# A^T and score rows by block transposes and GpSimd-issued DMAs, and the softmax tied to a later sum, in a two-layer graph kernel

## The chip, the cores and the metric

The kernel runs on one core of a Trainium2 chip. The metric is the time of one execution in device microseconds (us). Three runs of the kernel before gave 2418.76, 2420.62 and 2421.0; the median is 2420.62.

## What is computed

There are 128 graphs of 128 nodes with 512 features. Layer 0 is attention with three powers of a transition matrix; layer 1 weighs each node by a softmax over the nodes. Cut to what matters (`aw[:d]` and `aw[d:]` are the two halves of `aw`):

```python
h = relu(layernorm(x))                                   # layer 0
Xw = h @ Wv + bv
sj, si = Xw @ aw[:d], Xw @ aw[d:]
e = leaky_relu(sj[:, None, :] + si[:, :, None] + ab, 0.2)
alpha = A * exp(e)
T = alpha / (sum(alpha, -1) + 1e-12)
H, Xk = 0, h
for k in range(3):
    H = H + Xk @ Wk[k] + bk[k]
    Xk = T @ Xk
x = x + relu(H)
h = relu(layernorm(x))                                   # layer 1
q, k = split(h @ Wqk); v = h @ Wv1
w = (q * (A @ (k * mask))).sum(-1) * mask / sqrt(512)
x = x + softmax(w, over nodes)[:, :, None] * v
```

## The kernel before, in words

The graphs are worked two at a time (G = 2): 64 pairs, nodes on the 128 partitions. Both layers' large products are Strassen products of seven parts, where the two graphs of a pair are the two row halves. In layer 0 (`strassen0`, L356) a part is six matmuls of 256 columns; in layer 1 (`strassen1`, L387) it is two matmuls of 512 columns. The parts run in the order 1, 6, 7, 5, 2, 3, 4. They are summed in three PSUM banks (a, b and c in the code), and VectorE evicts intermediate sums between the parts (L366 to L381, and L398 to L408), each of which has to be read before a later part writes on into its bank. All matmuls of the two run from the helper at L346.

One turn of the loop (L476) holds layer 0 of pair p and layer 1 of pair p-1. In the middle of layer 0, `steps[0]` (called behind L369) brings in pair p+1: the feature transposes (`begin`, L271), `attention` (L274), and `finish` of layer 1 (L426) for the pair that ended last; `steps[1]` (called behind L374) brings `t_transposed` (L304). After layer 0 come `propagate` (L317, matmuls L325), the norm of layer 1's input, layer 1's product, `aggregate` (L411, matmul L417, sum L420), the left-hand sums (`left_sums`, L329), and at the end of the turn the norm and the score sums (L255) of pair p+2.

Three small jobs in that turn go through TensorE's transpose:

- `attention` needs the score of the neighbours as a row on every partition. `spread` (L97) transposes a column that is broadcast over 128 columns; there is one for each graph, into PSUM, from where VectorE reads it at L282.
- `attention` transposes A (L298); ScalarE scales the result by the mask at L302 on its way out of PSUM.
- `finish` spreads the column w of layer 1 in the same way (L97) and takes the maximum (L431) and two exponentials (L434) from it.

An operation goes to the engine that the code names; a scheduler decides the order on each engine when the program is built, by the order of the code and by when it takes operands to be ready. On the chip, each engine works down its own list. All loads and stores inside the loop are issued by SP, among them the pair's features written to DRAM and read back in blocks (hd, hv, L258 to L266), so that VectorE's 32x32 block transposes (L271) complete a transpose. GpSimd issues no DMA.

Buffers: four PSUM banks for the products and four for the rest, three sets of loaded inputs, two of most tiles in front, one of the tiles in `late`.

Of the kernel before, what the change touches and what calls it, by code (L numbers as in the profile page):

```python
# [8 lines left out]
FP = mybir.dt.float32  # L9
# [6 lines left out]
def kernel(  # L16
# [20 lines left out]
    nc = tc.nc  # L37
# [25 lines left out]

        return bass.AP(tensor=ap.tensor, offset=ap.offset + offset, ap=[[0, P], [1, n]])

    xg, ag = {}, {}

    def load(p):
        s = slice(p * G, (p + 1) * G)
        xg[p] = loads.tile([P, G, D], FP, name="xg")  # L70
        nc.sync.dma_start(xg[p], x[s].rearrange("b n d -> n b d"))
        ag[p] = loads.tile([P, G, N], FP, name="ag")
        nc.sync.dma_start(ag[p], adj[s].rearrange("b n m -> n b m"))


    nc.scalar.preload_act_table_set("natural_log_exp_and_others")
# [159 lines left out]
                                 bias=rs[:, 1, j:j + 1], scale=rs[:, 0, j:j + 1])  # L236
        return h

    H, HV, S, X, SX, AT, T, TT, X1, H2, X2, SX2 = ({} for _ in range(12))

    def norm0(p):

# [5 lines left out]
    def score_sums(p):  # L248

        h = H[p]  # L250
        s = S[p] = small.tile([P, G, 2], FP, name="s")
        for j in range(G):
            for a in range(2):
                junk = front.tile([P, D], FP, name="junk", bufs=1)
                nc.vector.scalar_tensor_tensor(junk, h[:, j, :], 1.0, u_bc[:, a, :], op0=OP.mult,  # L255
                                               op1=OP.mult, accum_out=s[:, j, a:a + 1])

    def by_blocks(h):  # L258

# [8 lines left out]
    def transposed(hv, dst):  # L268

        for j in range(G):  # L270
            nc.vector.transpose(dst[:, j].rearrange("p f (n b) -> p f n b", n=Q),  # L271
                                hv[:, j].rearrange("p n (f a) -> p f n a", f=Q))

    def attention(p):  # L274

        a, s = ag.pop(p), S.pop(p)
        pz = ps_t.tile([P, DC, P], FP, name="pt")
        for j in range(G):
            spread(pz[:, j, :], s[:, j, 0:1])
        z = front.tile([P, G, N], FP, name="z", bufs=1)  # L280
        for j in range(G):
            nc.vector.tensor_scalar(z[:, j, :], pz[:, j, :], s[:, j, 1:2], cz, op0=OP.add, op1=OP.add)  # L282
        nc.vector.scalar_tensor_tensor(z, z, 0.2, z, op0=OP.mult, op1=OP.max)
        ex = front.tile([P, G, N], FP, name="ex")
        nc.scalar.activation(ex, z, AF.Exp)
        d = small.tile([P, 2, G], FP, name="d")
        for j in range(G):
            nc.vector.scalar_tensor_tensor(ex[:, j, :], ex[:, j, :], 1.0, a[:, j, :], op0=OP.mult,
                                           op1=OP.mult, accum_out=d[:, 0, j:j + 1])
        nc.vector.tensor_scalar(d[:, 0], d[:, 0], 1e-12, None, op0=OP.add)  # L290
        nc.vector.reciprocal(d[:, 1], d[:, 0])
        t = T[p] = front.tile([P, G, N], FP, name="t")
        for j in range(G):
            nc.vector.tensor_scalar(t[:, j, :], ex[:, j, :], d[:, 1, j:j + 1], None, op0=OP.mult)

        pa = ps_t.tile([P, DC, P], FP, name="pt")
        for j in range(G):
            nc.tensor.transpose(pa[:, j, :], a[:, j, :], ident)  # L298
        AT[p] = front.tile([P, G, N], FP, name="aT", bufs=3)
        for j in range(G):  # L300
            b = p * G + j
            nc.scalar.activation(AT[p][:, j, :], pa[:, j, :], AF.Copy, scale=maskT[:, b:b + 1])  # L302

    def t_transposed(p):  # L304

        t, tt = T.pop(p), front.tile([P, G, 2, N], FP, name="tt")
        pt = ps_t.tile([P, DC, P], FP, name="pt")
        for j in range(G):
            nc.tensor.transpose(pt[:, j, :], t[:, j, :], ident)  # L309
        nc.scalar.copy(tt[:, :, 0, :], pt[:, :G, :])  # L310
        pt = ps_t.tile([P, DC, P], FP, name="pt")
        for j in range(G):
            nc.tensor.matmul(pt[:, j, :], t[:, j, :], tt[:, j, 0, :], start=True, stop=True)  # L313
        nc.scalar.copy(tt[:, :, 1, :], pt[:, :G, :])
        TT[p] = tt
# [40 lines left out]
    def strassen0(p, steps):  # L356

        product = products(SX.pop(p), right0)
        X.pop(p)
        lo, hi = bsum[:, :HD], bsum[:, HD:]  # L360
        hb = X1[p] = front.tile([P, G, D], FP, name="x1", bufs=3)
        s = front.tile([P, 4, HD], FP, name="s0", bufs=1)
        ba, bb, bc = (ps_m.tile([P, D], FP, name="pm") for _ in range(3))
        a, b, c = ba[:, :HD], bb[:, :HD], bc[:, :HD]
        product(ba, 1, True)
        nc.vector.tensor_add(s[:, 0], a, hi)  # L366
        nc.vector.tensor_add(s[:, 1], a, lo)
        product(bb, 6, True)
        nc.vector.tensor_add(s[:, 2], b, s[:, 1])  # L369
        steps[0]()  # L370
        product(bc, 7, True)
        product(bb, 5, False)
        nc.vector.tensor_add(s[:, 3], b, s[:, 0])
        nc.vector.tensor_add(hb[:, 1, HD:], c, s[:, 3])  # L374
        steps[1]()
        product(ba, 2, False)
        nc.vector.tensor_add(hb[:, 0, :HD], a, lo)
        product(bb, 3, False)
        nc.vector.tensor_add(hb[:, 0, HD:], b, s[:, 0])
        product(bc, 4, False)  # L380
        nc.vector.tensor_add(hb[:, 1, :HD], c, s[:, 2])  # L381
        xs = xg.pop(p)
        for j in range(G):
            nc.vector.scalar_tensor_tensor(hb[:, j, :], hb[:, j, :], 0.0, xs[:, j, :],
                                           op0=OP.max, op1=OP.add)

    def strassen1(p):  # L387

        product = products(SX2.pop(p), R1)
        X2.pop(p)  # L390
        yv = late["p"].tile([P, G, 2, 2, HD], FP, name="yv")
        o = [[yv[:, j, nh].rearrange("p k d -> p (k d)") for nh in range(2)] for j in range(G)]
        s = late["p"].tile([P, 3, D], FP, name="s1")
        a, b, c = (ps_m.tile([P, D], FP, name="pm") for _ in range(3))
        product(a, 1, True)
        nc.scalar.copy(s[:, 0], a)
        product(b, 6, True)
        nc.vector.tensor_add(s[:, 1], b, s[:, 0])  # L398
        product(c, 7, True)
        product(b, 5, False)  # L400
        nc.vector.tensor_add(s[:, 2], b, s[:, 0])
        nc.vector.tensor_add(o[1][1], c, s[:, 2])
        product(a, 2, False)
        nc.scalar.copy(o[0][0], a)
        product(b, 3, False)
        nc.vector.tensor_add(o[0][1], b, s[:, 0])  # L406
        product(c, 4, False)
        nc.vector.tensor_add(o[1][0], c, s[:, 1])  # L408
        return yv

    def aggregate(p, yv):  # L411

        h2, at = H2.pop(p), AT.pop(p)
        w = small.tile([P, 6, G], FP, name="w")
        for j in range(G):
            pa = ps_t.tile([P, D], FP, name="pt")
            nc.tensor.matmul(pa, at[:, j, :], h2[:, j, :], start=True, stop=True)  # L417
            junk = front.tile([P, D], FP, name="junk", bufs=1)
            b = p * G + j
            nc.vector.scalar_tensor_tensor(  # L420
                junk.rearrange("p (k d) -> p k d", k=2), pa.rearrange("p (k d) -> p k d", k=2),
                wscale[:, b:b + 1], yv[:, j, :, 0, :], op0=OP.mult, op1=OP.mult,
                accum_out=w[:, 0, j:j + 1])
        return w

    def finish(p, yv, w):  # L426

        pw = ps_t.tile([P, DC, P], FP, name="pt")
        for j in range(G):
            spread(pw[:, j, :], w[:, 0, j:j + 1])  # L430
        nc.vector.tensor_reduce(w[:, 1], pw[:, :G, :], AX.X, OP.max, negate=True)  # L431
        for j in range(G):
            ej = front.tile([P, N], FP, name="ej")
            nc.scalar.activation(ej, pw[:, j, :], AF.Exp, bias=w[:, 1, j:j + 1],  # L434
                                 accum_out=w[:, 2, j:j + 1])
        nc.vector.tensor_add(w[:, 3], w[:, 0], w[:, 1])
        nc.scalar.activation(w[:, 4], w[:, 3], AF.Exp)
        nc.vector.reciprocal(w[:, 5], w[:, 2])
        nc.vector.tensor_mul(w[:, 3], w[:, 4], w[:, 5])
# [29 lines left out]
    R1 = None  # L469
    ends = []  # L470

    def end():
        while ends:
            finish(*ends.pop())

    for p in range(NP + 1):  # L476
        if p < NP:
            if p + 1 < NP:
                n = p + 1
                steps = (lambda: (begin(n), attention(n), end()), lambda: t_transposed(n))  # L480
            else:
                steps = (end, lambda: None)
            strassen0(p, steps)
            if p + 1 < NP:
                propagate(p + 1)
# [7 lines left out]
        if p < NP:  # L493
            H2[p] = norm_relu(X1[p], "h2", late["p"])
            hv2 = by_blocks(H2[p])
        if p > 0:
            yv = strassen1(p - 1)
            w = aggregate(p - 1, yv)
        if p + 1 < NP:
            prepare0(p + 1)  # L500
        if p > 0:
            ends.append((p - 1, yv, w))
        if p < NP:
            X2[p] = late["p"].tile([P, G, 2, HC, N], FP, name="x2")
            transposed(hv2, X2[p].rearrange("p j h c n -> p j (h c) n"))
            a = {(j, kh): X2[p][:, j, kh:kh + 1].rearrange("p k c n -> p k (c n)")
                 for j in range(G) for kh in range(2)}
            SX2[p] = left_sums(a, late["p"], "sx2", [1, HD])
        if p + 2 < NP:
            norm0(p + 2)  # L510
            score_sums(p + 2)
    end()


# [23 lines left out]
```

## Time and profile before

| | |
|---|---|
| median of 3 runs | 2420.62 us |
| the profiled execution, its own time | 2420.37 us |
| its span in the profile | 2418.3 us |
| mean granted TensorE clock | 0.998 |
| VectorE (DVE) busy | 1786.8 us, 74% |
| ScalarE (ACT) busy | 650.5 us, 27% |
| GpSimd (POOL) busy | 0.7 us |
| DMA engines, 0 to 20 us, and 20 to 60 us | 0.89 and 0.71 busy |
| mean DMA rate | 91 GB/s |

The span runs from the first to the last instruction in the trace of one execution; the time of that execution is a little longer. PE is TensorE's matmuls and PEld its weight loads, which lie beside them. A line such as "L346 PE MATMUL pm<-t,sx" names the line of the code, the engine, the operation, and the tiles written and read. A row of the chain of waits names what the end of the run hung on at that time.

### The profile page before, as it was taken

How to read it: one execution, taken by the hardware profiler on the slowest of the kernel's cores; microseconds unless marked ns; L12 is line 12 of the kernel's file. 1: busy time of each engine (PE TensorE's matmuls, PEld its weight loads, DVE VectorE, ACT ScalarE, POOL GpSimd, SP SyncE). 2: the span in 40 equal slices, each digit the busy share in tenths (PEclk: the TensorE clock that was granted, in tenths of full speed). 3: DMA queues.
4: the chain of work that ended last, by engine and by line, in shares of the span. 5: the costliest groups of instructions: out<-in, count | busy, mean ns of one | idle time of the engine just before them, and what ended most of it. 6: DMA issues, size and time to landing. Idle time of an engine off the chain costs nothing.

```text
span 2418.3 us, 27245 instructions
## 1 busy us (share of the span) xinstructions
PE 2378.8 (98%) x9289; PEld 1694.5 (70%) x9289; DVE 1786.8 (74%) x4768; ACT 650.5 (27%) x1557; POOL 0.7 (0%) x6
## 2 busy tenths in 40 slices
PE   6999999999999999999999999999999999999997
PEld 4777677677676676776776776776766767767764
DVE  6777777777777777777777777777777777777764
ACT  3222222222222222223222222222222222232221
POOL 0000000000000000000000000000000000000000
PEclk9999999999999999999999999999999999999999
DMA  7233233233133233232332332332332332323311
GB/s 219 82 84 101 81 92 101 66 106 101 64 109 93 71 101 95 77 101 88 85 101 81 92 100 65 108 100 64 108 93 72 101 95 78 100 87 86 97 52 52
DMA packets 236986, 220.48 MB, mean 91 GB/s; under 512 B 14384, under 2 KB 170160, under 8 KB 236848
## 3 DMA queue, kind: packets, MB, share of 16 engines
q1 hardware_dynamic: 232624, 216.65, 30.5%
q10 hardware_dynamic: 4224, 2.10, 0.3%
q8 instruction: 73, 1.20, 0.2%
q14 instruction: 65, 0.53, 0.1%
HBM read 118.03 MB, written 100.66 MB: 90 GB/s over the span
## 4 chain that ended last, share of the span: by engine, by line
PE 96%; DVE 2%; DMA 1%; issue 0%; ACT 0%; SPq 0%; DVEq 0%; ACTq 0%
PE pm L346 79%; PE pt L325 9%; PE pt L417 4%; PE pt L97 1%; PE pt L313 1%; PE pt L298 1%; PE pt L309 1%; DMA bk_bc<-in_L_gnn_bk_dram 0%; DMA hd<-h 0%; DVE st L220 0%; DMA hv<-hd 0%; DMA w<-in_L_gnn_Wqk_dram 0%; DMA xg<-in_x_dram 0%; DVE x L271 0%; PE pm L208 0%
## 5 line engine op out<-in xcount | busy, mean ns | idle before, releaser
L346 PE MATMUL pm<-t,sx 128*128 128x256 f32 x2304 | 518.6, 380 | 1.4 <-DVE sx L333 1.4
L346 PEld LDWEIGHTS pm<-t,sx 128*128 128x128 f32 x2304 | 433.4, 190 | 57.4 <-DVE sx L333 2.0
L346 PE MATMUL pm<-b,x 128*128 128x256 f32 x1536 | 363.0, 380 | 0.0
L346 PE MATMUL pm<-f,sx 128*128 128x512 f32 x768 | 344.8, 598 | 0.3
L346 PEld LDWEIGHTS pm<-b,x 128*128 128x128 f32 x1536 | 282.6, 191 | 59.3 <-issue 29.6
L327 ACT COPY x<-pt 128x512 f32<-128x512 f32 x256 | 148.7, 581 | 500.6 <-PE pt L325 500.6
L346 PEld LDWEIGHTS pm<-f,sx 128*128 128x128 f32 x768 | 141.6, 191 | 193.7 <-issue 154.4
L346 PE MATMUL pm<-e,x 128*128 128x512 f32 x512 | 242.5, 596 | 6.5 <-DVE x L271 6.5
L325 PE MATMUL pt<-tt,h 128*128 128x256 f32 x1024 | 231.5, 379 | 0.0
L325 PEld LDWEIGHTS pt<-tt,h 128*128 128x128 f32 x1024 | 194.9, 190 | 26.2
L255 DVE SCALAR_TENSOR_TENSOR junk<-h,u_bc 128x512 f32<-128x512 f32 x256 | 176.4, 689 | 7.8 <-ACT h L235 0.9
L346 PE MATMUL pm<-b,sx 128*128 128x256 f32 x768 | 176.5, 379 | 0.0
L346 PE MATMUL pm<-t,x 128*128 128x256 f32 x768 | 176.2, 379 | 0.0
L235 ACT ACTIVATE h<-x,rs 128x512 f32<-128x512 f32 x128 | 97.2, 806 | 289.9 <-PE pt L417 277.1
L271 DVE STREAM_TRANSPOSE x<-hv 128x512 f32<-128x512 f32 x256 | 166.4, 688 | 6.6 <-DMA hv<-hd 5.7
L346 PEld LDWEIGHTS pm<-e,x 128*128 128x128 f32 x512 | 97.8, 191 | 102.8 <-issue 92.3
L346 PEld LDWEIGHTS pm<-t,x 128*128 128x128 f32 x768 | 146.2, 190 | 19.6
L346 PEld LDWEIGHTS pm<-b,sx 128*128 128x128 f32 x768 | 146.0, 190 | 19.5
L406 DVE TENSOR_TENSOR yv<-pm,s 128x512 f32<-128x512 f32 x64 | 44.3, 692 | 128.5 <-PE pm L346 128.5
L235 ACT ACTIVATE h<-xg,rs 128x512 f32<-128x512 f32 x128 | 97.2, 806 | 119.8 <-DVE rs L232 119.8
L417 PE MATMUL pt<-h,aT 128*128 128x512 f32 x256 | 120.5, 593 | 0.5 <-ACT h L235 0.5
L346 PE MATMUL pm<-e,sx 128*128 128x512 f32 x256 | 120.3, 592 | 0.0
(101 smaller groups left out, 2511.3 us busy)
## 6 DMA issues: line engine op xcount, KB each, us to landing
hd<-h SPq DMA_DIRECT2D x128, 512.0 KB, 3.1
hv<-hd SPq DMA_DIRECT2D x512, 128.0 KB, 3.3
xg<-in_x_dram SPq DMA_DIRECT2D x64, 512.0 KB, 3.6
out_dram<-x SPq DMA_DIRECT2D x64, 512.0 KB, 3.1
ag<-in_adj_dram SPq DMA_DIRECT2D x64, 128.0 KB, 3.0
w<-in_L_gnn_Wqk_dram ACTq DMA_DIRECT2D x8, 256.0 KB, 5.0
b<-in_L_gnn_Wk_dram SPq DMA_DIRECT2D x8, 256.0 KB, 3.4
wv_sb<-in_L_gnn_Wv_dram SPq DMA_DIRECT2D x4, 256.0 KB, 5.3
```

Source lines behind the costliest of these rows:

```text
L97: nc.tensor.transpose(dst, col.to_broadcast([P, P]), ident)
L235: nc.scalar.activation(h[:, j, :], src[:, j, :], AF.Relu, bias=rs[:, 1, j:j + 1], scale=rs[:, 0, j:j + 1])
L255: nc.vector.scalar_tensor_tensor(junk, h[:, j, :], 1.0, u_bc[:, a, :], op0=OP.mult, op1=OP.mult, accum_out=s[:, j, a:a + 1])
L271: nc.vector.transpose(dst[:, j].rearrange("p f (n b) -> p f n b", n=Q), hv[:, j].rearrange("p n (f a) -> p f n a", f=Q))
L298: nc.tensor.transpose(pa[:, j, :], a[:, j, :], ident)
L309: nc.tensor.transpose(pt[:, j, :], t[:, j, :], ident)
L313: nc.tensor.matmul(pt[:, j, :], t[:, j, :], tt[:, j, 0, :], start=True, stop=True)
L325: nc.tensor.matmul(pt[:, c].rearrange("p k n -> p (k n)"), h[:, j, at:at + P], tt[:, j].rearrange("p k n -> p (k n)"), start=True, stop=True)
L327: nc.scalar.copy(X[p][:, 1:3, j, kh].rearrange("p k c n -> p c k n"), pt)
L346: nc.tensor.matmul(bank[:, :r.shape[-1]], left[i][:, k, c * P:(c + 1) * P], r, start=(first and at == 0), stop=(at == len(chunks) - 1), sk ...
L406: nc.vector.tensor_add(o[0][1], b, s[:, 0])
L417: nc.tensor.matmul(pa, at[:, j, :], h2[:, j, :], start=True, stop=True)
```

## The change

Every load of a pair also reads A a second time, in blocks of 32x32 (`agb`), by four DMAs that GpSimd issues. One block transpose on VectorE turns it into A^T, and ScalarE scales that in place. The score column and layer 1's column w are kept in zeroed tiles of 128x32 (`cols`); a block transpose makes rows of them, two small DMAs put the rows into DRAM, and one DMA broadcasts them back to all partitions, all three issued by GpSimd (`spread_pair`). Pair 0's scores and the last pair's w still go through TensorE. `norm0` of pair p+2 moves ahead of layer 1's product, and its score sums into the middle of it. In layer 0, `attention` is called one part later (behind part 7's matmuls), `t_transposed` one part later (behind L377), and `finish` writes its maximum into the tile of layer 0's last intermediate sum, `s[:, 3]`, so that it comes behind L374, which reads that sum. Some tiles get one buffer instead of two, and the exponential is taken in place.

```diff
+        agb[p] = loads.tile([P, G, Q, S32], FP, name="agb", bufs=2)
+        v = adj[s].rearrange("g (q b) (c i) -> c b (g q) i", b=S32, i=S32)
+        for c in range(Q):
+            nc.gpsimd.dma_start(agb[p][c * S32:(c + 1) * S32].rearrange("p g q i -> p (g q) i"), v[c])
...
+    cols = [const.tile([P, S32], FP, name=f"col{i}") for i in range(6)]
+    for t in cols:
+        nc.gpsimd.memset(t, 0.0)
...
-        s = S[p] = small.tile([P, G, 2], FP, name="s")
+        s = S[p] = cols[p % 3]
...
+        PZ[p] = spread_pair(s, "pz", p > 0)
...
+    def spread_pair(col, name, by_dma):
+        if by_dma:
+            t = small.tile([P, S32], FP, name=f"{name}t", bufs=1)
+            nc.vector.transpose(t, col)
+            d = dram.tile([G, Q, S32], FP, name=f"{name}d")
+            for j in range(G):
+                nc.gpsimd.dma_start(d[j], t[j::S32])
+            dst = front.tile([P, G, N], FP, name=name, bufs=1)
+            nc.gpsimd.dma_start(dst.rearrange("p g n -> p (g n)"), bcast(d, 0, G * N))
+            return dst
+        pz = ps_t.tile([P, DC, P], FP, name="pt")
+        for j in range(G):
+            spread(pz[:, j, :], col[:, j:j + 1])
+        return pz[:, :G]
...
-        ex = front.tile([P, G, N], FP, name="ex")
+        ex = z
...
-        t = T[p] = front.tile([P, G, N], FP, name="t")
+        t = T[p] = front.tile([P, G, N], FP, name="t", bufs=1)
...
-        pa = ps_t.tile([P, DC, P], FP, name="pt")
-        for j in range(G):
-            nc.tensor.transpose(pa[:, j, :], a[:, j, :], ident)
         AT[p] = front.tile([P, G, N], FP, name="aT", bufs=3)
+        nc.vector.transpose(AT[p].rearrange("p g n -> p (g n)"),
+                            agb.pop(p).rearrange("p g q i -> p (g q i)"))
...
-            nc.scalar.activation(AT[p][:, j, :], pa[:, j, :], AF.Copy, scale=maskT[:, b:b + 1])
+            nc.scalar.activation(AT[p][:, j, :], AT[p][:, j, :], AF.Copy, scale=maskT[:, b:b + 1])
...
-        t, tt = T.pop(p), front.tile([P, G, 2, N], FP, name="tt")
+        t, tt = T.pop(p), front.tile([P, G, 2, N], FP, name="tt", bufs=1)
...
         product(bc, 7, True)
+        steps[1]()
         product(bb, 5, False)
         nc.vector.tensor_add(s[:, 3], b, s[:, 0])
         nc.vector.tensor_add(hb[:, 1, HD:], c, s[:, 3])
-        steps[1]()
+        end(s[:, 3, :G])
         product(ba, 2, False)
         nc.vector.tensor_add(hb[:, 0, :HD], a, lo)
+        steps[2]()
         product(bb, 3, False)
...
         nc.vector.tensor_add(o[1][1], c, s[:, 2])
+        if ahead < NP:
+            score_sums(ahead)
         product(a, 2, False)
...
-        nc.vector.tensor_reduce(w[:, 1], pw[:, :G, :], AX.X, OP.max, negate=True)
+        nc.vector.tensor_reduce(peak, pw, AX.X, OP.max, negate=True)
...
-                steps = (lambda: (begin(n), attention(n), end()), lambda: t_transposed(n))
+                steps = (lambda: begin(n), lambda: attention(n), lambda: t_transposed(n))
...
+        if p + 2 < NP:
+            norm0(p + 2)
         if p > 0:
-            yv = strassen1(p - 1)
+            yv = strassen1(p - 1, p + 2)
+        elif p + 2 < NP:
+            score_sums(p + 2)
+        if p > 0:
             w = aggregate(p - 1, yv)
...
-            ends.append((p - 1, yv, w))
+            ends.append((p - 1, yv, w, spread_pair(w, "pw", p < NP)))
...
-        if p + 2 < NP:
-            norm0(p + 2)
-            score_sums(p + 2)
```

More of the change, by code (lines that the diff above doesn't have):

```diff
@@ L64, in bcast @@
         return bass.AP(tensor=ap.tensor, offset=ap.offset + offset, ap=[[0, P], [1, n]])
-    xg, ag = {}, {}
+    xg, ag, agb = {}, {}, {}
     def load(p):
@@ L237, in norm_relu @@
         return h
-    H, HV, S, X, SX, AT, T, TT, X1, H2, X2, SX2 = ({} for _ in range(12))
+    cols = [const.tile([P, S32], FP, name=f"col{i}") for i in range(6)]
+    for t in cols:
+        nc.gpsimd.memset(t, 0.0)
+    H, HV, S, PZ, X, SX, AT, T, TT, X1, H2, X2, SX2 = ({} for _ in range(13))
     def norm0(p):
@@ L255, in score_sums @@
                 nc.vector.scalar_tensor_tensor(junk, h[:, j, :], 1.0, u_bc[:, a, :], op0=OP.mult,
-                                               op1=OP.mult, accum_out=s[:, j, a:a + 1])
+                                               op1=OP.mult, accum_out=s[:, a * G + j:a * G + j + 1])
+        PZ[p] = spread_pair(s, "pz", p > 0)
     def by_blocks(h):
@@ L272, in transposed, with attention @@
                                 hv[:, j].rearrange("p n (f a) -> p f n a", f=Q))
-    def attention(p):
-        a, s = ag.pop(p), S.pop(p)
+    def spread_pair(col, name, by_dma):
[8 more added lines that the diff above has]
+            return dst
         pz = ps_t.tile([P, DC, P], FP, name="pt")
         for j in range(G):
-            spread(pz[:, j, :], s[:, j, 0:1])
+            spread(pz[:, j, :], col[:, j:j + 1])
+        return pz[:, :G]
+    def attention(p):
+        a, s, pz = ag.pop(p), S.pop(p), PZ.pop(p)
         z = front.tile([P, G, N], FP, name="z", bufs=1)
         for j in range(G):
-            nc.vector.tensor_scalar(z[:, j, :], pz[:, j, :], s[:, j, 1:2], cz, op0=OP.add, op1=OP.add)
+            nc.vector.tensor_scalar(z[:, j, :], pz[:, j, :], s[:, G + j:G + j + 1], cz, op0=OP.add, op1=OP.add)
         nc.vector.scalar_tensor_tensor(z, z, 0.2, z, op0=OP.mult, op1=OP.max)
-        ex = front.tile([P, G, N], FP, name="ex")
+        ex = z
         nc.scalar.activation(ex, z, AF.Exp)
@@ L385, in strassen0, with strassen1 @@
                                            op0=OP.max, op1=OP.add)
-    def strassen1(p):
+    def strassen1(p, ahead):
         product = products(SX2.pop(p), R1)
@@ L413, in aggregate @@
         h2, at = H2.pop(p), AT.pop(p)
-        w = small.tile([P, 6, G], FP, name="w")
+        w = cols[3 + p % 3]
         for j in range(G):
@@ L422, in aggregate, with finish @@
                 wscale[:, b:b + 1], yv[:, j, :, 0, :], op0=OP.mult, op1=OP.mult,
-                accum_out=w[:, 0, j:j + 1])
+                accum_out=w[:, j:j + 1])
         return w
[L426 to L430, printed above, removed]
-        nc.vector.tensor_reduce(w[:, 1], pw[:, :G, :], AX.X, OP.max, negate=True)
+    def finish(peak, p, yv, ws, pw):
+        w = ws[:, :6 * G].rearrange("p (k g) -> p k g", g=G)
+        nc.vector.tensor_reduce(peak, pw, AX.X, OP.max, negate=True)
         for j in range(G):
             ej = front.tile([P, N], FP, name="ej")
-            nc.scalar.activation(ej, pw[:, j, :], AF.Exp, bias=w[:, 1, j:j + 1],
+            nc.scalar.activation(ej, pw[:, j, :], AF.Exp, bias=peak[:, j:j + 1],
                                  accum_out=w[:, 2, j:j + 1])
-        nc.vector.tensor_add(w[:, 3], w[:, 0], w[:, 1])
+        nc.vector.tensor_add(w[:, 3], w[:, 0], peak)
         nc.scalar.activation(w[:, 4], w[:, 3], AF.Exp)
@@ L470, with end @@
     ends = []
-    def end():
+    def end(peak=None):
         while ends:
-            finish(*ends.pop())
+            finish(small.tile([P, G], FP, name="peak") if peak is None else peak, *ends.pop())
     for p in range(NP + 1):
@@ L479 @@
                 n = p + 1
-                steps = (lambda: (begin(n), attention(n), end()), lambda: t_transposed(n))
+                steps = (lambda: begin(n), lambda: attention(n), lambda: t_transposed(n))
             else:
-                steps = (end, lambda: None)
+                steps = (lambda: None,) * 3
             strassen0(p, steps)
```

## The prediction

> **What bounds the kernel now.** I read the busy shares first, then the chain of waits over the whole span and over one pair, then VectorE's timeline of that pair, then the waits.
>
> ```profile
> PE 2378.8 (98%) x9289; PEld 1694.5 (70%) x9289; DVE 1786.8 (74%) x4768; ACT 650.5 (27%) x1557; POOL 0.7 (0%) x6
> ```
> ```profile
> PE 96%; DVE 2%; DMA 1%; issue 0%; ACT 0%; SPq 0%; DVEq 0%; ACTq 0%
> ```
>
> TensorE is busy all the time and is 96% of the chain that ends last. The chain over one pair:
>
> ```profile
> 1031.23 5.18 PE pm L346 x24
> 1036.41 0.22 PE pt L97 x2
> 1036.62 0.22 PE pt L298 x2
> 1036.84 0.22 PE pt L97 x2
> 1037.06 5.18 PE pm L346 x24
> 1042.24 0.22 PE pt L309 x2
> ...
> 1050.68 3.45 PE pt L325 x16
> 1054.13 12.07 PE pm L346 x28
> 1066.21 1.72 PE pt L417 x4
> ```
>
> Columns are start, length and what ran. There is no gap, so a pair costs what TensorE is given: from 1036.41 to 1073.11, where the next pair has the same L97 row, 36.70 us. The three 0.22 us rows are what the change removes.
>
> The other engine that matters is VectorE. In its timeline (start, mean length, operation, idle time before) I look at the first evictions of layer 1:
>
> ```profile
> 1042.28 0.42 DVE L373 TENSOR_TENSOR s<-pm,s 128x256 f32<-128x256 f32 x1 [0.91 <-PE pm L346]
> 1042.74 0.42 DVE L374 TENSOR_TENSOR x<-pm,s 128x256 f32<-128x256 f32 x1
> ...
> 1048.59 0.69 DVE L384 SCALAR_TENSOR_TENSOR x<-x,xg 128x512 f32<-128x512 f32 x1
> ...
> 1058.34 0.68 DVE L398 TENSOR_TENSOR s<-pm,s 128x512 f32<-128x512 f32 x1
> ```
>
> L398's input is ready when layer 1's second product ends, 1054.13 + 2 x 1.72 = 1057.57, but VectorE comes to it at 1058.34, with no idle time named before it. The waits say the same:
>
> ```profile
> PEld pm L346 <- DVE s L398: 38.8, 63, 1.0
> ```
>
> So TensorE's weight load already waits 0.6 us a pair there, and the matmul stream just escapes. VectorE is 74% busy on average, but late at this place.
>
> **The change, part by part.** I call S the start of a pair's layer-0 products in the chain (1031.23); one layer-0 product is 2.59 us, one of layer 1 1.725.
>
> *TensorE.* Two score transposes go for pairs 1 to 63, two softmax transposes for pairs 0 to 62, two of A^T for all 64: 126 + 126 + 128 = 380 by 0.109 (half of a 0.22 row), 41.3 us in all, 0.65 a pair. All of it stands on the chain. The period would be 36.05 and the run 2420.4 - 41.3 = 2379.1.
>
> *VectorE, what is added.* Per pair one 128x256 block transpose (half of L271's 0.65 pace: 0.33) and two 128x32 ones (about 0.1 each, the pace of the smallest operations). Reading the scores from SBUF instead of PSUM should bring L282 from 0.36 nearer to L294's 0.22 pace, about 0.3 back. The sum is +0.2 us on an engine with some 8 us idle a pair: nothing by itself.
>
> *VectorE, what is moved.* This costs. In the changed kernel's instruction order the softmax (L431 to L439, two L443) stands behind L374 where it stood before L373. It leaves VectorE's wait for product 5 and enters the stretch with no slack. Added up from starts in the rows above: product 5 ends at S + 10.36; L373 starts 0.04 later; L374 0.46 after that; the maximum (L431) 0.46 later, **S + 11.3**. L438 must wait for the two exponentials on ScalarE: 1.3 (in the tail L431 starts 2411.12, L438 2412.48). Then 0.11, two block transposes 1.25, L439 0.08, L377 0.34, three left sums 1.02, two L443 1.33 with the fourth left sum 0.34 between, L379 0.46: L384 starts at S + 17.5. From L384 to L398 it was 9.75; the fourth 768-wide sum (0.87) now comes later, so 8.9: L398 starts at S + 26.4, done S + 27.1. TensorE overwrites its operand at S + 22.23 + 5.18 - 0.16 = S + 27.25 (0.16: matmuls start that much ahead of the chain's stamps). It just fits.
>
> The next step doesn't. The score sums (L255) were behind L420; now one stands between L398 and L401, and needs the normed rows. L398 to the last scale: 0.60 + 0.07 + 0.10 + 0.85 (the moved sum) + 0.07 + 0.1 + 0.2 + 0.2 + 0.19 = 2.3; L235 on ScalarE 0.85; L255 0.61; L401 0.69: S + 30.9. Product 3 of layer 1 overwrites L401's operand at S + 30.7. TensorE waits **0.23 us a pair**. Each term is a row, but thirty are chained, so I hold it to +-0.35.
>
> *GpSimd's DMAs, per pair ten:* four of A (32 partitions x 8 runs each), twice two small stores to DRAM and twice a broadcast back. GpSimd issues no DMA in this trace, so its price has no row. The nearest is hv, of the same 32x8 shape:
>
> ```profile
> hv<-hd SPq DMA_DIRECT2D x512, 128.0 KB, 3.3
> ```
>
> SP's eight hv issues take 3.83 us, 0.48 each, and land 3.3 after the issue began, 2.85 after it ended. That is the low end. For the high end I take a queue that holds each issue as long as a transfer takes to land (ag: 3.0).
>
> Two results have a due time. The *score row*: its transpose ends at S - 2.5, then two stores, a landing, a broadcast, a landing. With issue price g: S - 2.5 + 3g + 5.7, at 0.48 S + 4.65. VectorE needs it 2.45 us (two L282, L283, exponential, two L288, L369) before product 5 starts at S + 7.77, so at S + 5.3, since L369 is queued behind L288 and product 5 waits for L369. The *softmax row*: its transpose ends at S + 1.4 (two L420, the A^T transpose, the small one); GpSimd then issues one A load, two stores, three A loads and the broadcast, 7g, and 2.85 to land: at 0.48 S + 7.6, at 1.0 S + 11.25. It is due at L431, S + 11.3. Behind L431 in VectorE's queue are both evictions above, and behind the exponentials in ScalarE's is L310's copy, which TensorE waits for: each us late is a us per pair. At 3.0 per issue it is 13.9 late, some 860 us over 62 pairs. I take at most 1.0, twice SP's row, because SP's is the only row of this shape, and keep the rest for the range.
>
> The Trainium skill speaks against the change. DMA: Bandwidth & Descriptors, section "Latency and other measured facts", gives a first byte after about 1 us for a DMA issued by GpSimd, against 0.6 for SP; no run here shows it yet. By that, the score row's two round trips come 0.8 later and miss their due time by 0.15, an estimated 9 us over the run; without it nothing. SBUF — State Buffer, section "Who interferes with whom", says that VectorE in some two-port operations blocks GpSimd for the whole instruction; at L294's 0.28 us, one such block on the softmax row would be an estimated 17 us if that row had no slack, and nothing if it has.
>
> *Other edits.* Single buffers for t, tt, z and the exponent in place: the former reader is done a period earlier, so nothing; if that cover went, 0.4 us (one L285). The later t transposes (behind product 2 instead of 5): t is ready by S + 9.5 and due at S + 12.95. The four A loads bring 1024 packets of 128 bytes a pair; the one small-packet row (q10: 0.3% of 16 engines over 4224 packets) makes 27 ns a packet, 1.7 us of 16 engines a pair that are 30% busy: hidden. In the first 60 us the DMAs are 71 to 89% busy and sixteen such loads come on top: 6.9 us of all engines, bounds 0 and +7, I take +4. The tail keeps its TensorE transposes.
>
> **Sum for the forecast:** 36.70 - 0.65 + 0.23 = 36.28, a gain of 0.42 on 62 pairs = 26 us; 2420.4 - 26 + 4 = **2398 us**. The profiled run (2420.37, span 2418.3 and 2.1 around it) is within 0.3 us of the median of 2420.62.
>
> **Rivals.**
> - *The full gain.* VectorE's chain is 0.25 shorter than I added: 2379 + 4 = 2383. For it: L398 escapes today. Against: the moved softmax.
> - *VectorE takes it all back.* The chain is 0.35 longer: period 36.63, about 2420. For it: 0.6 us of weight-load waits at that place already.
> - *The softmax row comes late (slower).* Place: L431, with VectorE and ScalarE queued behind it. It decides from 1.0 us per GpSimd issue, and the whole gain is gone at about 1.06, where the row is 0.42 late. At 1.3 it lands at S + 13.35, 2.05 late: 62 x (2.05 - 0.42) + 4 = +105, 2525 us. For it: seven issues and two landings in a row on one queue, no row of that queue, slack of a few tenths at twice SP's price. Against: SP's 0.48.
> - *The change doesn't do what it says*: excluded as far as the order goes; in the changed program no L97 row is left inside the loop before the last pair, and the maximum stands directly behind L374.
>
> **Chances.** Forecast 0.44, full gain 0.08, taken back 0.10, late row 0.38. What a measurement of this kernel can tell from no change is 0.2%, 5 us. Faster is the first two, 0.52; same 0.08; slower 0.40, with 0.02 of the taken-back case. The forecast's own range is 2380 to 2415 (62 x 0.35 below and above, less at the bottom where the full gain ends). The late row reaches from 2438 (1.1 us an issue) to beyond 2600 (1.5 and more); I keep it up to 2545 and leave out 0.13 above and 0.05 below 2380.
>
> **What would show it.** Right: L97 and L298 gone from the steady chain; period near 36.3; TensorE's idle time named by L401; L431 without a wait. Wrong: TensorE waiting on L369 (score row late), or VectorE idle before L431 on a DMA and ScalarE's L310 copy late (softmax row late), with GpSimd issues well over 1 us. No idle time on TensorE at all would prove the full gain. It would also be wrong if the start cost far more than 7 us.

## The result, and the profile after

The changed kernel takes **2503.15 us** (median of six runs, 2497.41 to 2506.34) where the kernel before takes 2419.61 beside it: a ratio of 1.034, 95% interval 1.033 to 1.036. The forecast of 2398 had the wrong sign. The time lies in the range, and the rival "the softmax row comes late" is what happened, though not through the price that I gave it.

In this table a turn runs from one pair's first `aggregate` matmul (L417 before, L442 after) to the next pair's, 61 of them from pair 0 to pair 61; the start is what lies ahead of pair 0's, the tail what follows pair 61's. All are read from TensorE's timeline of the profiled execution; that of the changed kernel took 2506.34 us, the longest of its six.

| us | start | mean turn | tail | span |
|---|---|---|---|---|
| before | 111.5 | 36.71 | 67.5 | 2418.3 |
| after | 124.1 | 37.83 | 72.5 | 2504.3 |
| difference | +12.6 | 61 x 1.12 = +68.4 | +5.0 | +86.0 |

The turns of before are alike. Those of after go from 36.3 to 42.6, with no pattern: they hang on something that varies. TensorE's busy share in the changed kernel's page:

```profile
PE 2386.1 (95%) x8909; PEld 1647.9 (66%) x8909; DVE 1784.4 (71%) x4958; ACT 659.4 (26%) x1557; POOL 371.3 (15%) x646
```

TensorE has 380 instructions less, as worked out, and yet is busy longer (2378.8 us before). Part of a wait seems to be counted as matmul time: in layer 1's product 3 (`pm<-e,sx`, see L401 in the prediction) a matmul takes 617 ns, 592 before. The chain of waits reaches back over only the last 141 us of this span, so I read the waits and one pair's timeline in its place. The waits (engine, line waited for, us in total, times, longest):

```profile
POOL pw L292 <- DMA pwd<-pwt: 175.0, 56, 4.9
DVE s L455 <- DMA pw<-pwd: 96.2, 59, 3.2
PE pt L334 <- ACT tt L331: 38.9, 47, 2.1
PEld pm L367 <- DVE s L421: 65.1, 62, 1.4
PE pm L367 <- DVE s L421: 15.1, 57, 0.6
```

VectorE waits at the maximum (L455, L431 before) for the broadcast softmax row, 1.6 us in nearly every pair. Behind it TensorE waits at two places: for ScalarE's copy of the transposed t (L331, L310 before, queued behind the exponentials) and for the first eviction of layer 1 (L421, L398 before). Both were named for this rival. One pair, GpSimd's timeline, then SP's, VectorE's and TensorE's:

```profile
1042.26 0.62 POOL L77 DMA_DIRECT2D agb<-in_adj_dram  x1 [0.17 <-DVE pwt L287]
1042.87 1.14 POOL L290 DMA_DIRECT2D pwd<-pwt  x2
1044.00 1.79 POOL L77 DMA_DIRECT2D agb<-in_adj_dram  x3
1048.84 0.59 POOL L292 DMA_DIRECT2D pw<-pwd  x1 [3.06 <-DMA pwd<-pwt]
```
```profile
1042.31 0.88 SPq L269 DMA_DIRECT2D hd<-h  x2
```
```profile
1051.12 0.42 DVE L395 TENSOR_TENSOR s<-pm,s 128x256 f32<-128x256 f32 x1 [3.17 <-PE pm L367]
1051.58 0.42 DVE L396 TENSOR_TENSOR x<-pm,s 128x256 f32<-128x256 f32 x1
1053.37 0.42 DVE L455 TENSOR_REDUCE s<-pw 128x2 f32<-128x256 f32 x1 [1.36 <-DMA pw<-pwd]
```
```profile
1055.11 0.71 PE L334 MATMUL pt<-tt,t 128*128 128x128 f32 x4 [0.34 <-ACT tt L331]
1068.99 1.98 PE L367 MATMUL pm<-f,sx 128*128 128x512 f32 x4 [0.25 <-DVE s L421]
```

S is 1040.72 here (layer 0's first matmul starts at 1040.56, and the chain's stamps are 0.16 later). GpSimd issues in 0.57 to 0.61 us each. But it then stands 3.06 us at L292 until the two stores of the row have landed, and the broadcast lands another 4.5 after its issue: S + 12.65, not S + 7.6. It was due at S + 11.3, so it is 1.35 late, and this turn is 37.42. What the queue was waiting for shows in the landing times (from issue, median):

```profile
pz<-pzd POOLq DMA_DIRECT2D x63, 128.0 KB, 3.4
pw<-pwd POOLq DMA_DIRECT2D x63, 128.0 KB, 4.5
pzd<-pzt POOLq DMA_DIRECT2D x126, 0.5 KB, 1.6
pwd<-pwt POOLq DMA_DIRECT2D x126, 0.5 KB, 4.9
```

Two rows of one size by the same code: the score row's 0.5 KB stores (pzd) land in 1.6 us, the softmax row's (pwd) in 4.9. Beside the second, and not the first, SP issues its two stores of normed features (hd, L269, 512 KB each).

**Theory:** the softmax row is late because its stores land late beside SP's two large stores; VectorE and ScalarE are queued behind it. **Rivals:** the score row is the bound; the four loads of A on GpSimd's queue are what holds the row; the new order makes VectorE late whatever the rows do.

### The profile page after: what moved, and what is told of

It is laid out like the page before. It is cut to its first block, busy times and chain, and to the rows that moved or that the text cites. A ratio compares the mean times of both kernels' runs of the same rounds, so it can differ in the third digit from the quotient of the medians.

```text
span 2504.3 us, 27652 instructions
## 1 busy us (share of the span) xinstructions
PE 2386.1 (95%) x8909; PEld 1647.9 (66%) x8909; DVE 1784.4 (71%) x4958; ACT 659.4 (26%) x1557; POOL 371.3 (15%) x646
## 5 line engine op out<-in xcount | busy, mean ns | idle before, releaser
L367 PE MATMUL pm<-t,sx 128*128 128x256 f32 x2304 | 512.9, 381 | 8.2 <-DVE s L390 6.6
L367 PEld LDWEIGHTS pm<-t,sx 128*128 128x128 f32 x2304 | 440.0, 191 | 70.2 <-DVE s L390 7.8
L367 PE MATMUL pm<-f,sx 128*128 128x512 f32 x768 | 357.4, 602 | 15.1 <-DVE s L421 15.1
L367 PE MATMUL pm<-b,x 128*128 128x256 f32 x1536 | 352.6, 379 | 0.0
L367 PEld LDWEIGHTS pm<-b,x 128*128 128x128 f32 x1536 | 292.0, 190 | 66.3 <-issue 29.7
L290 POOL DMA_DIRECT2D pzd<-pzt x126 | 72.6, 578 | 1703.2 <-DVE pzt L287 1693.8
L367 PE MATMUL pm<-b,sx 128*128 128x256 f32 x768 | 186.5, 379 | 0.0
L458 ACT ACTIVATE ej<-pw,s 128x128 f32<-128x128 f32 x124 | 48.7, 394 | 471.5 <-DVE s L455 471.5
L367 PEld LDWEIGHTS pm<-e,x 128*128 128x128 f32 x512 | 97.9, 192 | 111.5 <-issue 92.8
L395 DVE TENSOR_TENSOR s<-pm,s 128x256 f32<-128x256 f32 x64 | 27.2, 425 | 190.5 <-PE pm L367 190.5
L77 POOL DMA_DIRECT2D agb<-in_adj_dram x256 | 154.1, 607 | 22.3 <-DVE aT L319 7.3
```

The costliest lines, as they stand in the source:

```text
L77: nc.gpsimd.dma_start(agb[p][c * S32:(c + 1) * S32].rearrange("p g q i -> p (g q) i"), v[c])
L290: nc.gpsimd.dma_start(d[j], t[j::S32])
L367: nc.tensor.matmul(bank[:, :r.shape[-1]], left[i][:, k, c * P:(c + 1) * P], r, start=(first and at == 0), stop=(at == len(chunks) - 1), sk ...
L458: nc.scalar.activation(ej, pw[:, j, :], AF.Exp, bias=peak[:, j:j + 1], accum_out=w[:, 2, j:j + 1])
```

## The experiments

All edits are to the changed kernel, unless said otherwise. "Landing" is that of the softmax row's stores, the median from issue. Times are medians of four to ten runs; turn and landing are of the one profiled execution (in experiment 1 the fastest of ten, 2410.8 us, with the slowest at 2418.8).

| edit | us | ratio to before (95%) | mean turn | landing |
|---|---|---|---|---|
| none | 2503.2 | 1.034 (1.033 to 1.036) | 37.83 | 4.9 |
| 1 softmax row by TensorE | 2416.9 | 0.998 (0.997 to 0.999) | 36.47 | – |
| 2 score row by TensorE | 2475.0 | 1.023 (1.022 to 1.025) | 37.46 | 3.9 |
| 3 loads of A for A^T by SP | 2452.2 | 1.013 (1.012 to 1.015) | 36.91 | 4.4 |
| 4 maximum behind a later sum | 2459.7 | 1.017 (1.015 to 1.018) | 37.08 | 5.2 |
| 5 SP stores layer 0's features first | 2500.6 | 1.034 (1.032 to 1.037) | 37.99 | 3.1 |
| 6 one of SP's two stores cut | 2424.2 | 1.002 (1.001 to 1.003) | 36.48 | 3.6 |
| 7 both cut | 2402.6 | 0.993 (0.991 to 0.995) | 36.25 | 2.2 |
| 8 pair 1's score row by TensorE | 2494.1 | 1.030 (1.028 to 1.033) | 37.68 | 4.8 |
| 9 experiments 1 and 8 together | 2412.6 | 0.998 (0.997 to 0.999) | 36.47 | – |
| 10 A^T alone, new order | 2409.1 | 0.996 (0.995 to 0.998) | 36.49 | – |
| 11 A^T alone, old order | 2409.0 | 0.996 (0.994 to 0.997) | 36.49 | – |
| 12 a new order alone | 2443.1 | 1.010 (1.008 to 1.012) | 37.17 | – |

### 1, 2: which row

```diff
-            ends.append((p - 1, yv, w, spread_pair(w, "pw", p < NP)))
+            ends.append((p - 1, yv, w, spread_pair(w, "pw", False)))
```


> The softmax row of every pair goes through TensorE again (two transposes, 0.22 us a pair back); score row and A^T stay on GpSimd. Theory (the softmax row lands late, VectorE and ScalarE stand behind it): the wait at the maximum disappears, a pair falls from 37.8 us (mean over the loop) to 36.3 to 36.6, the run to about 2410 to 2430. Rival 1 (the late row is harmless, the work moved behind layer 0's last sum is what costs): stays within 20 us of 2503. Rival 2 (the score row holds product 5): stays at 2503 or above, with TensorE waiting for the eviction before product 5.

2416.9, most turns 36.38. Giving 0.22 us a pair back to TensorE took 86 us off the run: the softmax row's path holds the loss.

```diff
-        PZ[p] = spread_pair(s, "pz", p > 0)
+        PZ[p] = spread_pair(s, "pz", False)
```


> The score row of every pair goes through TensorE again (0.22 us a pair back); the softmax row and A^T stay on GpSimd. Theory (softmax row): VectorE still waits at the maximum, a pair stays above 37 us, the run at 2480 to 2520. Rival 2 (score row): TensorE stops waiting before product 5 and the run falls below 2440.

2475.0, a little below the theory's 2480, far above the rival's 2440. The score row isn't what bounds the changed kernel. It has a share, though: without its DMAs the landing is 3.9.

### 3: the loads of A on GpSimd's queue

```diff
-            nc.gpsimd.dma_start(agb[p][c * S32:(c + 1) * S32].rearrange("p g q i -> p (g q) i"), v[c])
+            nc.sync.dma_start(agb[p][c * S32:(c + 1) * S32].rearrange("p g q i -> p (g q) i"), v[c])
```


> All rows as in the changed kernel, but the four block loads of A are issued by SP, so that nothing stands between the stores and the broadcast on GpSimd's queue. Theory (the stores land 4.9 us after issue because loads of A are queued around them, against 1.6 for the score row's stores): the softmax row's stores land within 2.5 us, the row is there by S + 8.5, VectorE has no wait at the maximum, a pair is 36.2 to 36.7 us, the run 2405 to 2435. Rival 1 (moved VectorE work): stays near 2500. Rival 2 (the score row): stays near 2490. Rival 3 (GpSimd's DMAs are slow in themselves): the stores still land after 4 us or more, the run is above 2470.

2452.2 lies between the two. The row is issued sooner, and a few turns come down to 35.98. But GpSimd still stands waiting for the stores with nothing of its own left between them and the broadcast (GpSimd's timeline, then SP's):

```profile
1016.57 1.11 POOL L290 DMA_DIRECT2D pwd<-pwt  x2 [0.31 <-DVE pwt L287]
1022.60 0.57 POOL L292 DMA_DIRECT2D pw<-pwd  x1 [4.92 <-DMA pwd<-pwt]
```
```profile
1016.62 0.91 SPq L269 DMA_DIRECT2D hd<-h  x2
```

So the loads of A hold the row up somewhat on GpSimd's queue, but that queue isn't why two 0.5 KB stores take over 4 us. The loads themselves are still made at that time, by SP; this run doesn't take them away.

### 4: more time for the row

```diff
-        end(s[:, 3, :G])
         product(ba, 2, False)
         nc.vector.tensor_add(hb[:, 0, :HD], a, lo)
         steps[2]()
         product(bb, 3, False)
         nc.vector.tensor_add(hb[:, 0, HD:], b, s[:, 0])
+        end(s[:, 0, :G])
```


> All three transposes stay off TensorE; the softmax is tied one eviction pair later, behind the sum after product 3 (S + 15.6 instead of S + 10.4). Theory (only the due time of the softmax row matters): a row that lands at S + 12.6 has 3 us to spare, VectorE's wait at the maximum and ScalarE's late copy are gone, a pair takes 36.0 to 36.4 us, the run 2390 to 2415. Rival 1 (the amount of VectorE work between there and layer 1 decides, wherever the row is): a pair above 37, the run above 2460. Rival 2 (score row): the run above 2460, TensorE waiting before product 5.

2459.7: 44 us won, less than the theory said, and nearer to its second rival. The wait at the maximum has gone, and the next one in line has come up, the score row's (waits of this kernel):

```profile
DVE z L304 <- DMA pz<-pzd: 169.6, 63, 5.6
PE pm L367 <- DVE s L390: 45.1, 61, 3.6
```

L390 is the eviction (L369 before) that the prediction put behind the score row, due at S + 5.3. The broadcast of that row lands in 4.2 us here, against 3.4.

### 5: moving one of SP's stores out of the way

```diff
-            hv2 = by_blocks(H2[p])
         if p + 2 < NP:
             norm0(p + 2)
+        if p < NP:
+            hv2 = by_blocks(H2[p])
```


> By the second theory the softmax row's stores land late (4.4 us after issue even with no load of A around them, against 1.6 for the score row's) because they are issued in the same half microsecond as SP's two stores of h, 512 KB each. Here one of the two is issued a part of a turn earlier, since the norm that it stores stands ahead in the program. Theory: the stores land after 2.5 to 3.7 us, the row comes 1 us earlier or more, a pair falls from 37.8 to 36.5 to 37.2, the run to 2430 to 2470. Rival (GpSimd's stores are late for a reason of their own, or the loads of A do it): 4.4 to 4.9 us as before and a run within 15 us of 2503.

The landing fell to 3.1 as expected, the total not at all. The store of layer 0's features now goes out before the score row's stores, and these take 3.0 us where they took 1.6. TensorE waits at L390:

```profile
PE pm L367 <- DVE s L390: 55.5, 60, 2.4
```

The lateness went from one row to the other. That speaks for the theory's cause, but the total had been expected at 2430 to 2470, and that failed.

### 6, 7: the suspected cost taken away

What 3 to 5 left open was whether SP's stores are the cause or only stand beside it. Here they are cut to 8 of 128 nodes, one and then both, while the order on TensorE, VectorE, ScalarE and GpSimd stays as it is. `kept[part]` is one DRAM tile that all pairs share, `first` the pair that fills it.

The last two lines are in experiment 7 only. In both, the other nodes keep the values of the first pair, so these kernels leave out part of the work:

```diff
-        HV[p] = by_blocks(h)
+        HV[p] = by_blocks(h, "a")
...
-        hd = dram.tile([G, P, D], FP, name="hd")
-        nc.sync.dma_start(hd.rearrange("g n d -> n g d"), h)
...
+            hd = kept[part]
+        n = P if part is None or first else 8
+        nc.sync.dma_start(hd[:, :n].rearrange("g n d -> n g d"), h[:n])
...
-            hv2 = by_blocks(H2[p])
+            hv2 = by_blocks(H2[p], "b")
```


> The changed kernel, but of the normed features of layer 0 (h of the pair two ahead) only 8 of the 128 nodes are stored to DRAM in each turn after the first; the blocks read back hold the first pair's values for the rest, so the values differ. The order on every engine is unchanged; of the two 512 KB stores that SP issues in the half microsecond before the softmax row's stores, one is left. Theory (the row's two 0.5 KB stores land late because they stand beside SP's two stores): their landing falls from 4.9 us to about 3, the row lands near its due time of S + 11.3, the mean turn falls from 37.83 to 36.3 to 36.9 and the run to 2410 to 2455. Rival 1 (the landing is late because of the other loads on GpSimd's own queue, the blocks of A, or the blocks read back by SP): landing stays above 4, run above 2470. Rival 2 (the lateness of VectorE in the new order, not the row): landing falls but the run stays above 2450.

> As the kernel with one store left, with the second store (normed features of layer 1) cut to 8 of 128 nodes as well: 16 small rows per store in place of 512 KB, orders unchanged. Theory: the row's stores land in about 1.6 to 2.2 us, as the score row's do; the softmax row is there by S + 9.5, VectorE's wait at the maximum is gone, the mean turn is 36.05 to 36.4 and the run 2390 to 2425 (the start stays about 12 us longer). Rival 1 (own queue): landing above 4, run above 2470. Rival 2 (the new order's VectorE lateness): landing falls, but the turn stays near the 37.1 of the order alone, run above 2440.

Both came as the theory has it: landing 4.9, 3.6, 2.2 us and run 2503, 2424, 2403 with two, one and none of the stores. With none, VectorE's wait at the maximum (L464 in that file) is down from 96.2 us to 6.4, and GpSimd's at L301 (L292) from 175.0 us to 22.9:

```profile
POOL pw L301 <- DMA pwd<-pwt: 22.9, 10, 3.5
DVE s L464 <- DMA pw<-pwd: 6.4, 10, 1.3
```

VectorE's timeline of a pair of that kernel has the maximum straight behind the two sums:

```profile
1038.71 0.42 DVE L404 TENSOR_TENSOR s<-pm,s 128x256 f32<-128x256 f32 x1 [3.15 <-PE pm L376]
1039.17 0.42 DVE L405 TENSOR_TENSOR x<-pm,s 128x256 f32<-128x256 f32 x1
1039.63 0.42 DVE L464 TENSOR_REDUCE s<-pw 128x2 f32<-128x256 f32 x1
```

46 of the 62 turns are then 36.09 to 36.11. The edit has a wider effect than one landing: 62 MB less are moved over the run (183.7 for 245.6), and the blocks of A land in 2.8 us for 4.2. So it shows that SP's stores make the row late; it doesn't show by which path. The blocks read back (hv) and the loads of A are still there, and beside them the row's stores land in 2.2 us.

### 8, 9: the start

```diff
-        PZ[p] = spread_pair(s, "pz", p > 0)
+        PZ[p] = spread_pair(s, "pz", p > 1)
```


> Only pair 1's score row goes through TensorE as pair 0's does. The changed kernel reaches the end of its second turn 12.6 us later than before (125.98 against 113.39). Theory for that: ScalarE's exponential for pair 1 waits for the score row, and the copies of the layer 1 weights are queued behind it; then 6 to 10 us go and the run is about 2495. Rival (the loads of A crowd the first transfers): no change, within 3 us of 2503.

> The changed kernel with the softmax row by TensorE's transposes in all pairs and pair 1's score row by TensorE as well; the other score rows and A^T stay with the DMAs. Theory: the steady turn of the softmax row by TensorE (36.38), and 5 to 9 us less at the start: 2405 to 2413. Rival (the start is bound by something else than pair 1's score row once the softmax row is by TensorE): 2415 to 2419.

The totals came as expected, 2494.1 and 2412.6. The reason holds for the first only: its start is 115.8 us, 8.3 shorter. In the trace of the changed kernel TensorE waits at the start 6.1 us for a copy of weights (L204) that is queued on ScalarE behind pair 1's exponential, which waits for pair 1's score row; with that row by TensorE the wait is 0.5. But the second has a start of 117.8, no shorter than the 117.3 of experiment 1, and the two intervals overlap: there this edit gains nothing that these runs can tell. The traces show why. In experiments 1 and 7 pair 1's score row still goes by DMA, but its exponential starts at 45.0 us, 49.9 in the changed kernel, and the wait at L204 is 0.5 there too. So it costs only where that row is late; why it is late in the changed kernel and not in those two stays open.

### 10, 11, 12: what the other parts are worth

```diff
-        PZ[p] = spread_pair(s, "pz", p > 0)
+        PZ[p] = spread_pair(s, "pz", False)
...
-            ends.append((p - 1, yv, w, spread_pair(w, "pw", p < NP)))
+            ends.append((p - 1, yv, w, spread_pair(w, "pw", False)))
```


> Only A^T by block loads and a block transpose, both rows through TensorE, in the new order. Theory: 0.22 us a pair less than the order alone, a pair 36.4 to 36.5, the run 2400 to 2415, 10 to 18 us below the run with the order alone. Rival (the loads of A disturb the other transfers and cost by that): at or above the run with the order alone.

The other is the kernel before with A^T by block loads and nothing else of the change, except the exponential in place:

```diff
-        for j in range(G):
-            nc.tensor.transpose(pa[:, j, :], a[:, j, :], ident)
+        nc.vector.transpose(AT[p].rearrange("p g n -> p (g n)"),
+                            agb.pop(p).rearrange("p g q i -> p (g q i)"))
```


> The kernel before, with only A^T by four block loads of A that GpSimd issues and a block transpose on VectorE (and the exponential in place, for room); order, score row and softmax row as before. TensorE gives up 64 x 0.22 = 14 us. Theory (A^T is nearly free and its gain full wherever VectorE is not late): 2405 to 2413 with a turn of 36.48. Rival (0.33 us more on VectorE ahead of layer 0's evictions, in the stretch where it is late already, takes it back): turn 36.6 to 36.8, run 2415 to 2428.

2409.1 and 2409.0, with turns of 36.47 and 36.48 for most: TensorE's 36.70 less the 0.22 of A^T, to a hundredth, in either order. These two are the fastest versions with the whole computation, 0.4% below before. A^T is the part of the change that pays in full, as its loads have most of a turn to land. The score row by DMA besides (experiments 1 and 9) brings the usual turn to 36.38, 0.09 less of the 0.22 hoped for, but the run to 2416.9 and 2412.6: it doesn't pay.

In the last one all three jobs stay with TensorE and only the order changes (the two edits of experiment 10, and A^T's old lines put back):

> Only the new order (norm and score sums ahead, attention and the t transposes one part later, softmax tied behind the last intermediate sum); all six transposes of a pair are back on TensorE and GpSimd issues nothing. Theory: no row can be late, TensorE sets the pace, a pair 36.7 us, the run 2412 to 2432. Rival 1 (the moved VectorE work costs): a pair above 37.3, the run above 2455.

2443.1, a turn of 37.10 for most: worse than the theory's 36.7, and short of its rival's 37.3; neither came. But it isn't the order of the changed kernel. Its VectorE has all four 768-wide sums ahead of layer 1's first eviction, which is L418 there:

```profile
1028.76 0.95 DVE L353 TENSOR_TENSOR sx<-x,sx 128x768 f32<-128x768 f32 x1
...
1029.77 0.68 DVE L418 TENSOR_TENSOR s<-pm,s 128x512 f32<-128x512 f32 x1
```

In experiment 10, as in the changed kernel, the last of them comes behind that eviction:

```profile
1020.51 0.69 DVE L421 TENSOR_TENSOR s<-pm,s 128x512 f32<-128x512 f32 x1
...
1021.26 0.95 DVE L356 TENSOR_TENSOR sx<-x,sx 128x768 f32<-128x768 f32 x1
```

In experiment 12 TensorE's weight loads wait 55.4 us for that eviction, in experiment 10 0.4 us. One sum of 0.95 us on the wrong side of it is then the likely cause of the 0.40 a turn (37.10 for 36.70); no run moved that sum alone. It fits the small slack that the prediction gave this place. The rival that lays the loss on the order is refuted for the changed kernel by 1, 7 and 10, not by 12.

## Why the prediction was wrong, by its steps

- *TensorE, 0.65 us a pair:* right. In the last full turn VectorE has no norm and no score sums of a later pair to do; it is 36.64 before and 35.99 in experiment 7. So 0.06 of the 36.70 seems to have been waiting already, where the prediction read no gap.
- *VectorE's chain:* its instants were right to 0.3 us. In the pair of experiment 7 shown above (S = 1028.31) L384's successor starts at S + 17.6 (S + 17.5 worked out), L398's at S + 26.2 (26.4), and L401's is done at S + 30.6 (30.9). What it costs TensorE was put at 0.23 a pair and is about 0.1: a usual turn there is 36.10, against 35.99, and four matmuls of 617 ns for 592 make the same.
- *GpSimd's issue price:* it was bounded by 0.48 and 1.0, and is 0.57 to 0.61. The rival's threshold of 1.0 was never reached.
- *Score row:* in time, but not by its sum. It is there at S + 4.05 in the pair shown, due S + 5.3; S + 4.65 had been worked out, and 0.8 later held possible. Its stores land in 1.6 us from issue, where the sum had 3.3.
- **Softmax row: this is the step that failed.** "GpSimd then issues one A load, two stores, three A loads and the broadcast, 7g, and 2.85 to land." Two things are wrong in it. First, the broadcast waits for the landing of the two stores. The score row's sum had both landings, this one had only the last, as if the three loads of 0.6 us covered the first. By my own 3.3 us from issue to landing, the row would be there at S + 2.7 + 3.3 + 3.3 = S + 9.3, still in time, so that alone did not turn the sign. Second, the landings: 4.9 and 4.5 us instead of 3.3 each, 2.8 together. That brings it to about S + 12.1; with the start of the broadcast's issue, 0.5 after the landing, it is the S + 12.65 measured.
- *What a late row costs:* right. Due at S + 11.3, "each us late is a us per pair": 36.10 + 96.2/62 = 37.65, measured 37.83. The 0.18 that is left has no single row.
- *DMA traffic:* "hidden", since the engines are 30% busy. As a mean that is so (0.36 after, between 1000 and 1500 us). The row's stores are issued within 1.2 us of 1 MB of SP's, and there the mean tells nothing. I looked at when GpSimd would issue, never at what SP issues at that time, though SP's hd row was in the page.
- *The start:* +4, bounded by 0 and 7, was +12.6. With A^T's loads alone it is 2 to 5 (experiments 11 and 10). In the changed kernel's trace 6.1 us are the wait for ScalarE's copy of weights behind pair 1's late score row, and eight slow matmuls right behind it take 2.2 more (last section); the remainder has no row.
- *The tail:* nothing was expected; it is +5.0. The chain that ended last has the softmax row of the pair before the last in it:

```profile
2467.51 4.54 DMA pwd<-pwt
2472.08 0.47 issue
2472.57 3.68 DMA pw<-pwd
```

That pair's row still goes through DRAM, and its stores and the broadcast take over 8 us with the end behind them: TensorE's wait ahead of the last pair's layer 1 is 11.8 us, 6.5 before. With the row by TensorE (experiment 1) the tail is 67.1.

The rival came true by another route than the one its chance of 0.38 was argued from, so that its 2525 us at 1.3 an issue lies near the 2503 measured is luck. What was wrong was to price it by the issue and to take the landing as known from rows of other DMAs at other times. With the stores cut the run is 2402.6, some 5 us from the forecast of 2398. That is partly errors that offset each other: the cost at L401 was 0.13 a pair less than put down, the start 2 and the tail 3 us more, and some turns are still longer than 36.10.

The Trainium skill, in DMA: Bandwidth & Descriptors, section "Issuing engines are not separate DMA queues", says that DMAs started by different engines run on the same 16 DMA engines and interleave. The runs fit that, without showing the engines themselves: GpSimd's 0.5 KB store lands in 4.9, 3.6 or 2.2 us with two, one or none of SP's large ones beside it. Another queue bought the row no passage of its own.

What stays open: why the softmax row's broadcast still lands in 4.4 us when SP's stores are cut, where the score row's takes 3.2. SP reads the blocks back (hv) at that time, which was not taken away in any run.

## What to carry to other kernels

A result that goes through DRAM costs two landings in a row. Here the first depended on what another queue had in flight at that moment (1.6 to 5.2 us for the same 0.5 KB); list every queue's issues around the instant before pricing one. Give such a path to operands with most of a turn to spare (A^T here: its full 0.22 us a pair), and not to one that VectorE and ScalarE stand in line behind. If a job on the bound engine costs 0.22 us a pair and its replacement can be a microsecond late, the job is cheap where it is.

## What the hardware showed unexpectedly

- A 0.5 KB store lands in 1.6 us when SP issues no large store near it, and in 4.9, in experiment 4 in 5.2, beside two of 512 KB (medians).
- GpSimd's issue takes nearly the same time for all three kinds here: 0.57 us for a 0.5 KB store, 0.585 for a 128 KB broadcast, 0.607 for the 32x8 blocks.
- Behind a long wait TensorE is slower for a while. At the start of the changed kernel eight matmuls take 5.87 us behind the 6.07 us wait, and 3.70 without one; the granted clock is 0.50 from 50 to 53 us and 0.73 from 53 to 57. In experiment 4, behind a wait of 3.65 us there, they take 5.40. Behind waits of 0.51 (experiments 1 and 7) they take 3.70.

```profile
40.59 3.70 PE L212 MATMUL pm<-wt,wt 128*128 128x512 f32 x8
...
50.80 5.87 PE L212 MATMUL pm<-wt,wt 128*128 128x512 f32 x8 [6.07 <-ACT wt L204]
```
